# Where the transposes of a part stand in the first step of a graph attention layer

## The chip, the cores and the metric

The kernel runs on one core of a Trainium2 chip. A core has five engines that run beside each other and wait for each other through semaphores: TensorE (PE, matmuls and transposes), VectorE (DVE), ScalarE (ACT), GpSimd (POOL) and SyncE (SP, which issues most of the transfers). The metric is the time of the whole program on the device in microseconds, the median of several runs. Beside it there is one profiled execution, from which all rows of the trace come.

## The reference

The input is a table `x` of N = 3327 nodes with 256 features and a sparse weighted adjacency `adj`. A normalised and rectified copy h of x goes through two steps. In each, attention sums rows with the weights of a nucleus (top-p) softmax, and the adjacency diffuses a second copy:

```python
R = S + eye(N);  R = R / R.sum(-1)
Z = 0;  Xf = Xa = h
for n in range(2):
    q, k = Xa @ W1.T @ W2.T, Xa @ W3.T
    p = softmax(q @ k.T)                     # N x N
    mask = the largest p of a row, until their sum reaches 0.9
    A = p * mask / (p * mask).sum(-1)
    Xf = R @ Xf
    Xa = A @ Xa
    Z = Z + Xf @ U1[n].T + Xa @ U2[n].T
out = x + layernorm(h + Z)
```

Everything is float32.

## The kernel before

**Tiles.** The nodes are padded to 26 tiles of 128 rows (NT = 26). A tile of one step needs its row of weights, 128 x 3328 numbers in one of several buffers `e`. For tile t the work is, in order:

- `weights`: the queries (`project`, pq L526 and L528), the logits against all keys (pl L567) and their Exp on ACT (e L571 and L575).
- `measured`: on ACT, two long passes over e (ja L600) and small operations in columns of `g`, which guess a threshold.
- `settle`: on DVE, w (L700), the largest values of segments (L705), their merging, and at last the mask, which overwrites e with the kept weights (L734).
- `Sums`: the masked e is transposed in groups of four 128 x 128 blocks, and each group is multiplied with the rows of the table and added up in `pa`.
- in the first step `first_end`: the result times U2 (pz L889), its copies xw (L890) and sv (L892), and the next step's keys and queries (`prep`, pk L487).

Beside it the adjacency is read (`listed`: at L810, fm L811), the few neighbours of a row are found (`packed`, `gathered`: pb, po, lo, index), POOL gathers their rows (ac L859, xg L868), and `spread` multiplies them (pr L876).

**Sums.** A tile has PARTS = 7 groups, six of four blocks and one of two. `turn(g, made)` transposes groups until group g + ahead is done: PE writes a block of PSUM `pt` (L779), ACT copies it to SBUF as `eT` (L781). `sum(g)` multiplies group g (pa L793). After a tile's seventh group ACT takes pa out (xa L800). There are three buffers of eT. PSUM has two buffers of pt, and these serve pk, pq, pb, po, pg and the transposes of results as well; pa and pr have one buffer each.

**The order of the work.** The loop near the end of the kernel writes down one order for all engines. Its passes i go over the tiles, and each pass has seven parts k. In a part, the letters of `PLAN[step][k]` say which piece of which generator comes next:

```python
PLAN = (("mdsssa", "mdsssa", "edawwp", "sda", "mpdea", "mdgawwq", "emdgq"), ...)
LATE = (1, 4)
```

m is `measured` for tile i+1, d is `settle` for tile i, s is `spread` for tile i-2, e is `first_end` for tile i-2, w and q are `weights` of tiles ahead, a is `listed`, p is `packed`, g is `gathered`. With LATE = 1 in the first step, part k of pass i sums group 7(i-1) + k - 1. So parts 1 to 6 sum the first six groups of tile i-1, and part 0 sums the seventh of tile i-2. What is left of the generators is run at the end of a pass.

PE, ACT and DVE are tied to the order of this text: a dependency of each instruction on the one before it on its engine is added after the loop (IN_ORDER). SP and POOL are not in that list; their queues are ordered by the framework's planner.

Of the kernel before, what the change touches and what calls it, by code (L numbers as in the profile page):

```python
# [22 lines left out]
NT = (N + P - 1) // P  # L23
# [299 lines left out]
SQG, SQK = ((c[0], c[1] / (2 * c[0]), c[2] - c[1] ** 2 / (4 * c[0])) for c in (PG, PK))  # L323
HALF = NT // 2
PARTS = -(-NT // 4)
AHEAD = (1, 2)
COUNTED = [t for t in range(NT - 2) if t % 2 == 0]
EARLY = (11, 18, NT)
FIRST = 8 * P
# [14 lines left out]
def guess_graph_layer(ctx, tc, x, adj, w1t, w2t, w3t, u1t, u2t, ln_g, ln_b, out, flag):  # L344
# [207 lines left out]
    def weights(step, t, live, known=True):  # L552

        r = dict(Z=rec[:, step, 3, t : t + 1])
        qT, r["ms"] = yield from project(step, t, law=known)
        yield
        r["e"] = e = es[(2, 3, 0, 1, 4, 5)[t % 6] if step else t % 4]
        r["za"] = za = small.tile([P, CUT + 1], F32, tag="za", name="za")
        live[step, t] = r
        w = HALF * P  # L560
        wd = w // CUT
        for n in range(CUT):
            c = n * wd
            pl = ps_l.tile([P, 2, 512], F32, tag="pl", name="pl")
            for a in range(2):
                p = slice(a * DA, (a + 1) * DA)
                PE.matmul(pl[:, a, :wd], qT[p, :],  # L567
                          keys[step][p].rearrange("p a b -> p (a b)")[:, c : c + wd],
                          start=True, stop=True)
            if n < CUT - 1:  # L570
                S.activation(e.rearrange("p (a n) -> p a n", a=2)[:, :, c : c + wd], pl[:, :, :wd],  # L571
                             AF.Exp, accum_out=za[:, n : n + 1])
                yield
            else:
                S.activation(e.rearrange("p (a n) -> p a n", a=2)[:, :, c : w - 1], pl[:, :, : wd - 1],  # L575
                             AF.Exp, accum_out=za[:, n : n + 1])
                S.activation(e[:, w - 1 : w], pl[:, 0, wd - 1 : wd], AF.Exp, accum_out=za[:, n + 1 :])
# [110 lines left out]
    def measured(step, r):  # L688
        return measured_twice(r) if step else measured_once(r)
# [52 lines left out]
    def prove(step):  # L742
        v8, t, tn, Z = (rec[:, step, k, :] for k in range(4))
        ok = small.tile([P, NT], F32, tag="cum", name="ok", bufs=1)
        o2 = small.tile([P, NT], F32, tag="dr", name="o2", bufs=1)
        V.tensor_tensor(ok, v8, t, ALU.is_lt)
        V.tensor_tensor(o2, tn, t, ALU.is_lt)
        V.tensor_tensor(ok, ok, o2, ALU.mult)
        for a, c, op in ((tn, 0.0, ALU.is_gt), (t, 0.5 * BIG, ALU.is_lt),
                         (Z, 1.0e-30, ALU.is_gt), (Z, BIG, ALU.is_lt)):  # L750
            V.scalar_tensor_tensor(ok, a, c, ok, op, ALU.mult)
        V.tensor_scalar(ok, ok, 0.5, None, ALU.is_lt)
        n = N - (NT - 1) * P
        f = small.tile([P, 1], F32, tag="f", name="f")
        V.tensor_reduce(f, ok[:, : NT - 1], AX.X, ALU.add)
        V.tensor_tensor(fl, fl, f, ALU.add)
        V.tensor_tensor(fl[:n], fl[:n], ok[:n, NT - 1 :], ALU.add)
        if step == 0:
            V.tensor_scalar(ok, lists[:, :, LIST - 1], 0.0, None, ALU.is_gt)
            V.scalar_tensor_tensor(ok, ends, float(P), ok, ALU.is_gt, ALU.add)  # L760
            V.tensor_reduce(f, ok, AX.X, ALU.add)
            V.tensor_tensor(fl, fl, f, ALU.add)
# [121 lines left out]
    def first_end(t):  # L884
        aT = transposed(live.pop(("r", t)))
        yield
        pz = ps_r.tile([P, 2 * D], F32, tag="pr", name="pz")
        for c in range(ND):
            PE.matmul(pz, aT[:, c, :], u2[:, c].rearrange("p n d -> p (n d)"), start=c == 0, stop=c == ND - 1)  # L889
        S.copy(xw[:, t, :], pz[:, D:])  # L890
        sv = row.tile([P, D], F32, tag="sv", name="sv", bufs=2)
        V.tensor_tensor(sv, pz[:, :D], x0[:, t, :], ALU.add)  # L892
        nc.sync.dma_start(sx[t], sv)
        yield
        yield from prep(1, aT, t)
# [32 lines left out]
    def run(work, n=99):  # L928
        for _ in range(n):
            next(work, None)  # L930

    def returned(work):
        while True:
            try:
                next(work)
            except StopIteration as end:
                return end.value[1]
# [52 lines left out]
    def spread(step, t):  # L990
        rr = rrs[:, t : t + 1]
        own = row.tile([P, D + 1], F32, tag="own", name="own", bufs=2)
        nc.sync.dma_start(*((own[:, :D], vx[:, t, :]) if step else (own, bx[:, t, :])))
        s1 = row.tile([P, D], F32, tag="s1", name="s1", bufs=4)
        nc.sync.dma_start(s1, (sx if step else ax)[t])
        a, w = acs.pop(t), D + 1 - step
        pr = yield from diffuse(a, xgs.pop(t), own[:, :w], w)
        if step == 0:
            nc.sync.dma_start(cx[t], a.rearrange("p k r -> p (k r)"))
        yield  # L1000
        if step == 0:
            V.reciprocal(rr, pr[:, D : D + 1])
        V.scalar_tensor_tensor(s1, pr[:, :D], rr, s1, ALU.mult, ALU.add)  # L1003
        if step == 0:
            nc.sync.dma_start(vx[:, t, :], s1)
        else:
            live["f", t] = s1
# [20 lines left out]
    for step in range(2):  # L1028
        sums = Sums(step, live, xw if step else x0, AHEAD[step])

        for i in range(-1, NT + 2):
            if step == 0 and i == NT - 3:
                begun = [weights(1, t, live, False) for t in range(3)]
            if step == 1 and i == -1:
                run(begun[0])
                prove(0)
                for e in es[4:]:
                    G.memset(e[:, N:NP], 0.0)
            work.update(
                n=work["m"],  # L1040
                c=work["d"],
                d=settle(step, i, live[step, i]) if valid(i) else none,
                m=measured(step, live[step, i + 1]) if valid(i + 1) else none,
                s=spread(step, i - 2 + 2 * step) if valid(i - 2 + 2 * step) else none,
                w=later.pop((step, i + 2), none),
                e=first_end(i - 2) if step == 0 and valid(i - 2) else none,
                a=lister if step == 0 and i else none,
                p=packed(i + 1) if step == 0 and i >= 0 and valid(i + 1) else none,
                g=none if not valid(i + 2 * step) else refetch(i + 2) if step else gathered(i),
                b=none, q=none, v=proof() if step and i == NT else none,  # L1050
            )
            if i >= 0 and valid(i + 3):
                later[step, i + 3] = weights(step, i + 3, live)
                work["q"] = itertools.islice(later[step, i + 3], 2)
            if step == 0 and i >= NT - 2 and i < NT + 1:

                work["w"] = itertools.islice(begun[i - NT + 2], CUT - 1)
            if step == 0 and i >= NT - 3 and i < NT:
                work["q"] = itertools.islice(begun[i - NT + 3], 1)
            if i == -1:  # L1060
                work["w"] = itertools.chain(begun[1], begun[2])
            if step == 0 and i < 1:
                work["b"] = itertools.islice(product, EARLY[i + 2] - EARLY[i + 1])
            if step == 1 and i == -1:
                work["g"] = itertools.chain(refetch(0), refetch(1))
            for k in range(PARTS):
                g = PARTS * (i - 1) + k - LATE[step]
                summing = valid(g // PARTS)
                if summing:
                    sums.turn(g, min(i, NT - 1))  # L1070
                for c in "bb" + (LAST.get(i, PLAN[1]) if step else PLAN[0])[k]:
                    next(work[c], None)
                if summing:
                    ended = sums.sum(g)
                    if ended and step == 0:
                        live["r", ended[0]] = ended[1]
                    elif ended:
                        work["f"] = finish(ended[0], live.pop(("f", ended[0])), ended[1])
            for c in "cnwqsepgb" if step else "dmwqsepgb":
                run(work[c])  # L1080
            if step == 0 and i == NT:
                moments(1)
                for t in range(3):
                    live[1, t]["ms"] = returned(project(1, t, queries=False))
# [50 lines left out]
```

## Time and profile before

| what | value |
|---|---|
| median of 9 runs | 1559.59 us (1552.86 to 1566.1) |
| the profiled execution | 1566.31 us, its span 1564.5 us |
| PE busy over the span | 1332.0 us, 85% |
| DVE busy | 1230.9 us, 79% |
| ACT busy | 1104.6 us, 71% |
| POOL busy | 1003.7 us, 64% |
| mean granted clock of TensorE | 0.945 |

The first step's tiles run until about 900 us; then comes the second step. In a row of the trace the line names the source, `out<-in` the tiles it writes and reads, and x the number of instructions. A float32 matmul appears as two records, so a sum of four blocks is `x8`; a transpose is one record. The brackets at the end of a row give the idle time of the engine before it and what ended that. Ends of matmuls are modelled, so rows that follow each other on PE overlap by some tenths of a microsecond.

### The profile page before, as it was taken

To read this page: it belongs to the slowest core of one execution; us is meant where nothing else is said; L and a number is where in the kernel's file an instruction comes from. 1 tells how busy PE (TensorE), PEld (TensorE's weight loads), DVE (VectorE), ACT (ScalarE), POOL (GpSimd) and SP (SyncE) were. 2 spreads that over 40 slices of the span, in tenths; PEclk is the share of its full clock that TensorE was granted. 3 is DMA by queue.
4 is the path that set the end of the run, shared out by engine and by line. 5 is a ranking of instruction groups with operands and counts; after the bars stand their busy time and mean duration, and the time that the engine had idled before them with its cause. 6 is when DMAs were issued, how large, how long until landed. Compare 5 with 4: busy or idle time off the path is not lost.

```text
span 1564.5 us, 22648 instructions
## 1 busy us (share of the span) xinstructions
PE 1332.0 (85%) x6495; PEld 997.5 (64%) x6495; DVE 1230.9 (79%) x3837; ACT 1104.6 (71%) x2476; POOL 1003.7 (64%) x1489
## 2 busy tenths in 40 slices
PE   5857788988988988989999946989989998998886
PEld 3523666666766666767767724767767667676675
DVE  4457789779779778779787229989888899898894
ACT  5527566766766766766775368988988988988951
POOL 6312466555566555565575166888888888888851
PEclk9978899998999999998999978999999999999998
DMA  7554344343444444344332231221221221222200
GB/s 218 166 161 134 102 130 121 109 122 117 111 128 120 116 117 116 112 127 120 110 88 81 60 88 31 72 75 55 74 72 50 82 64 58 82 60 63 81 18 20
DMA packets 97687, 149.81 MB, mean 96 GB/s; under 512 B 15985, under 2 KB 60528, under 8 KB 97552
## 3 DMA queue, kind: packets, MB, share of 16 engines
q1 hardware_dynamic: 78400, 104.00, 21.7%
q0 software_dynamic: 16640, 42.69, 11.0%
q10 hardware_dynamic: 2512, 1.57, 0.4%
q8 instruction: 54, 0.88, 0.2%
q14 instruction: 81, 0.66, 0.2%
HBM read 120.93 MB, written 27.28 MB: 95 GB/s over the span
## 4 chain that ended last, share of the span: by engine, by line
PE 33%; POOL 23%; ACT 19%; DVE 11%; issue 8%; DMA 4%; another core or an unknown queue 1%; SPq 0%; ACTq 0%; POOLq 0%; DVEq 0%
PE pa L793 14%; ACT ja L600 8%; POOL xg L868 8%; POOL g L678 4%; PE pt L779 4%; PE pr L876 4%; PE pl L567 4%; DMA at<-in_adj 3%; ACT e L571 3%; ACT eT L781 2%; PE pz L889 2%; DVE e L734 2%; DVE fm L811 1%; PE pk L487 1%; POOL rstd L468 1%
## 5 line engine op out<-in xcount | busy, mean ns | idle before, releaser
L781 ACT COPY eT<-pt 128x512 f32<-128x512 f32 (+1 forms) x364 | 201.9, 556 | 225.2 <-PE pt L779 136.6
L793 PE MATMUL pa<-x,eT 128*128 128x256 f32 x1352 | 356.0, 408 | 5.3 <-ACT eT L781 3.1
L793 PE MATMUL pa<-xw,eT 128*128 128x256 f32 x1352 | 331.1, 387 | 30.5 <-ACT xa L800 30.0
L859 POOL DMA_INDIRECT ac<-in_adj,index x130 | 173.6, 1335 | 243.0 <-DVE mq L541 158.6
L600 ACT ACTIVATE ja<-e,g 128x3328 uint8<-128x3328 f32 x106 | 325.8, 3074 | 0.1
L793 PEld LDWEIGHTS pa<-xw,eT 128*128 128x128 f32 x1352 | 249.3, 191 | 92.9 <-ACT xa L800 35.0
L793 PEld LDWEIGHTS pa<-x,eT 128*128 128x128 f32 x1352 | 263.7, 203 | 61.2 <-issue 16.5
L705 DVE MAX8 cand<-w 128x8 f32<-128x168 f32 (+1 forms) x1040 | 251.3, 319 | 0.0
L779 PE MATMUL pt<-ident,e 128*128 128x128 f32 x1144 | 181.4, 279 | 39.7 <-DVE e L734 24.0
L868 POOL DMA_INDIRECT xg<-bx,index x130 | 178.8, 1375 | 47.5 <-issue 33.8
L779 PEld LDWEIGHTS pt<-ident,e 128*128 128x128 f32 x1144 | 144.9, 145 | 79.2 <-issue 32.1
L567 PE MATMUL pl<-k,qT 64*128 64x416 f32 x832 | 185.5, 550 | 4.4 <-ACT qT L531 3.9
L700 DVE SCALAR_TENSOR_TENSOR w<-e,g 128x3328 f32<-128x3328 f32 x44 | 164.0, 3727 | 0.7
L876 PE MATMUL pr<-xg,ac 128*128 128x257 f32 (+1 forms) x520 | 138.3, 389 | 23.4 <-DVE s L1003 20.1
L811 DVE TENSOR_REDUCE fm<-at 128x4 f32<-128x512 f32 (+1 forms) x182 | 115.9, 638 | 53.7 <-DMA at<-in_adj 50.8
L868 POOL DMA_INDIRECT xg<-vx,index x130 | 128.5, 989 | 43.8 <-issue 36.9
L734 DVE SCALAR_TENSOR_TENSOR e<-e,rec 128x3328 f32<-128x3328 f32 x40 | 147.1, 3678 | 0.0
L571 ACT ACTIVATE e<-pl 128x832 f32<-128x832 f32 x132 | 113.4, 867 | 8.1 <-PE pl L567 6.7
L876 PEld LDWEIGHTS pr<-xg,ac 128*128 128x128 f32 x520 | 91.0, 195 | 34.1 <-DVE s L1003 20.4
L567 PEld LDWEIGHTS pl<-k,qT 64*128 64x128 f32 x832 | 70.8, 188 | 50.7 <-issue 42.1
L712 DVE MAX8 bb<-cand 128x8 f32<-128x160 f32 x286 | 92.8, 324 | 6.4
L892 DVE TENSOR_TENSOR sv<-pz,x 128x256 f32<-128x256 f32 x26 | 11.0, 421 | 97.3 <-ACT xw L890 94.4
(226 smaller groups left out, 2226.4 us busy)
## 6 DMA issues: line engine op xcount, KB each, us to landing
at<-in_adj SPq DMA_DIRECT2D x156, 256.0 KB
cx<-ac SPq DMA_DIRECT2D x26, 384.0 KB
ac<-cx SPq DMA_DIRECT2D x26, 384.0 KB
bx<-e SPq DMA_DIRECT2D x26, 128.5 KB
own<-bx SPq DMA_DIRECT2D x26, 128.5 KB
x<-in_x SPq DMA_DIRECT2D x13, 256.0 KB
xr<-in_x SPq DMA_DIRECT2D x26, 128.0 KB
ax<-e SPq DMA_DIRECT2D x26, 128.0 KB
```

Source lines behind the costliest of these rows:

```text
L567: PE.matmul(pl[:, a, :wd], qT[p, :], keys[step][p].rearrange("p a b -> p (a b)")[:, c : c + wd], start=True, stop=True)
L571: S.activation(e.rearrange("p (a n) -> p a n", a=2)[:, :, c : c + wd], pl[:, :, :wd], AF.Exp, accum_out=za[:, n : n + 1])
L600: S.activation(ja, e, f, bias=guess, scale=sign, accum_out=total)
L700: V.scalar_tensor_tensor(w, e, col(16), e, ALU.is_lt, ALU.mult, accum_out=d2)
L705: V.max(cand[:, 8 * s : 8 * s + 8], w[:, s * SEG : min(NP, (s + 1) * SEG)])
L734: V.scalar_tensor_tensor(e, e, at(1), e, ALU.is_ge, ALU.mult, accum_out=ra)
L779: PE.transpose(pt[:, j, :], e[:, (j0 + j) * P : (j0 + j + 1) * P], ident)
L781: S.copy(eT[:, :w, :], pt[:, :w, :])
L793: PE.matmul(self.pa, eT[:, c - 4 * k, :], self.xa[:, j, :], start=c == 0, stop=c == NT - 1)
L859: G.indirect_dma_start(out=ac[:, k, :], out_offset=None, in_=rows, in_offset=bass.IndirectOffsetOnAxis(ap=index[:, t, k : k + 1], axis=0), ...
L868: G.indirect_dma_start(out=xg[:, k, :w], out_offset=None, in_=rows, in_offset=bass.IndirectOffsetOnAxis(ap=index[:, t, k : k + 1], axis=0))
L876: PE.matmul(pr[:, :w], ac[:, k, :], own if k == KT - 1 else xg[:, k, :w], start=k == 0, stop=k == KT - 1)
```

## The change

In the first step the call of `turn` moves from the beginning of a part to behind the letters of the part, directly in front of the part's sum, and the transposes run two groups ahead of the sum and no longer one. In the second step both stay as they are. At the end of a pass, what is left of the generators now comes after both the transposes of the next tile's first group and the sum.

```diff
-AHEAD = (1, 2)
+AHEAD = (2, 2)
...
             for k in range(PARTS):
                 g = PARTS * (i - 1) + k - LATE[step]
                 summing = valid(g // PARTS)
-                if summing:
+                if summing and step:
                     sums.turn(g, min(i, NT - 1))
                 for c in "bb" + (LAST.get(i, PLAN[1]) if step else PLAN[0])[k]:
                     next(work[c], None)
+                if summing and not step:
+                    sums.turn(g, min(i, NT - 1))
                 if summing:
                     ended = sums.sum(g)
```

## The prediction

> **What bounds the kernel now.** I read the page first, then sums over the steady part of the first step (200 to 900 us), then who waited for whom there, then the chain of waits through a tile, and last the rows of single engines.
>
> ```profile
> span 1564.5 us, 22648 instructions
> PE 1332.0 (85%) x6495; PEld 997.5 (64%) x6495; DVE 1230.9 (79%) x3837; ACT 1104.6 (71%) x2476; POOL 1003.7 (64%) x1489
> 200.00:900.00 700.00, 626.94 (x3075) 476.15 (x3073) 552.44 (x1762) 458.19 (x1115) 400.94 (x510) 0.95 0.39 111
> L487 PE MATMUL pk<-xT,wk x100: 275/275/582, 208.5 to 896.0; 128*128 128x128 f32 x100
> ...
> DVE sv L892 <- ACT xw L890: 94.4, 15, 9.9
> ACT eT L781 <- PE pt L779: 92.0, 57, 5.2
> ACT eT L781 <- remote: 27.8, 10, 5.2
> PE pq L526 <- ACT eT L781: 39.8, 20, 2.9
> ```
>
> The page's second line has the busy shares of the whole span. The third line, from the view by windows, gives busy time in a stretch of 700 us: PE 627, DVE 552, ACT 458, POOL 401, at a granted clock of 0.95. No engine fills the stretch; PE has 73 us left. The fourth line, from the view of one source line, gives the cadence: four key matmuls per tile, so 25 tiles and 24 intervals from 208.5 to 896.0 us, 28.6 us each. The waits go in a ring: ACT waits for PE's transposes, PE for ACT's copies, DVE for ACT. Such a ring is shortened only by what stands in it, and the chain of waits shows it (start, length, what):
>
> ```profile
> 459.96 1.73 PE pa L793 x8
> 461.69 0.44 PE pt L779 x4
> 462.13 3.22 PE pz L889 x4
> ...
> 466.06 2.75 issue
> ...
> 469.01 0.26 ACT xw L890
> ...
> 472.17 0.85 ACT e L571 x2
> ...
> 474.40 0.71 PE pk L487 x4
> ```
>
> PE's sums and transposes lead up to ACT's long pass over a tile (L600, most of the 2.75 us called issue), then come xw, the Exp copies, and through mq the next tile's keys (pk) on PE. Call the seven groups of transposes of a tile T0 to T6 and their sums S0 to S6. Today's PE order in a tile is pk, S5 of the tile before, T0, S6 of the tile before, T1, S0, T2, S1, T3, S2, T4, pz, S3, T5, po, pl, pq, S4, T6, with the small products between. In the single rows of PE (one sum of four f32 matmuls is eight records) and ACT it looks like this:
>
> ```profile
> 532.59 0.71 PE L487 MATMUL pk<-xT,wk 128*128 128x128 f32 x4 [1.73 <-ACT mq L535]
> 533.14 1.89 PE L793 MATMUL pa<-x,eT 128*128 128x256 f32 x8
> ...
> 545.80 1.89 PE L793 MATMUL pa<-x,eT 128*128 128x256 f32 x8
> 547.53 0.60 PE L779 MATMUL pt<-ident,e 128*128 128x128 f32 x4
> 547.97 1.88 PE L889 MATMUL pz<-u,xT 128*128 128x512 f32 x4
> ...
> 551.41 0.60 PE L779 MATMUL pt<-ident,e 128*128 128x128 f32 x4
> ...
> 548.22 0.59 ACT L781 COPY eT<-pt 128x512 f32<-128x512 f32 x1 [1.63 <-issue]
> 548.70 3.07 ACT L600 ACTIVATE ja<-e,g 128x3328 uint8<-128x3328 f32 x1
> 551.77 0.36 ACT L890 COPY xw<-pz 128x256 f32<-128x256 f32 x1
> 555.90 0.59 ACT L781 COPY eT<-pt 128x512 f32<-128x512 f32 x1 [3.77 <-remote]
> ```
>
> ACT stands idle for 1.63 us until T4 is through, and T4 had to let S2 (545.80) pass. The long pass L600 stands behind the copy of T4 in ACT's queue, though it doesn't need it. The last row is a second thing: T5 ended at 552.01 (551.41 and 0.60), and its copy began 3.9 us later, with ACT idle for 3.77. PE's word that T5 is done came late.
>
> **The change part by part.** *Nothing is added or taken away*: the same transposes, copies and sums, no DMA, no new tile. SP and POOL get no instruction, and DVE keeps its order. On PE each T moves in front of one S. The new order is pk, T0, S5 before, T1, S6 before, T2, S0, T3, S1, T4, S2, pz, T5, S3, po, pl, pq, T6, S4. On ACT the copies change places with two small things only: the eviction xa now follows T1's copy, and the moments' copy gt follows T0's.
>
> *What is gained.* Between pk and the long pass, PE now has to do everything it did before except S2. So T4 comes one sum earlier, 1.73 us by the chain (1.89 by the row, whose end overlaps the next group). The copy of T4, L600 and, through xw, sv and mq, the next pk follow. The 1.63 us of ACT's idle time before T4's copy is the same amount seen from the other side. Is the gain given back within the tile? S2 falls behind T4, and xw also needs pz: T4 to the end of pz is 1.73 + 1.88 = 3.6 us, while the copy and L600 take 0.59 + 3.07 = 3.7 us. They come out level, so pz just doesn't take over. After xw, the gap to pk is ACT's (Exp, Ln and copies); T6 and S4 lie under it.
>
> *24 intervals of 1.73 us are 41.5 us.* Both ends: 0, if the late word sets the pace, and 73 us, PE's idle time in the stretch.
>
> *T6 before S4* makes T6 wait for ACT's copy of po earlier than it did, with S4 behind it. pk needs ACT's mq, which comes after two Exp copies (from 472.17 to pk at 474.40 in the chain, 2.2 us), and S4 needs 1.73 us: hidden. Without that cover it would cost 1.73 us a tile.
>
> *T0 before S5* puts a wait for DVE's mask (L734) ahead of a sum; behind it queue S5, the pr products and T1. The mask's rows:
>
> ```profile
> 527.50 0.42 DVE L892 TENSOR_TENSOR sv<-pz,x 128x256 f32<-128x256 f32 x1 [6.80 <-ACT xw L890]
> 528.43 3.68 DVE L734 SCALAR_TENSOR_TENSOR e<-e,rec 128x3328 f32<-128x3328 f32 x1
> ...
> 172.32 1.89 PE L793 MATMUL pa<-x,eT 128*128 128x256 f32 x8
> 181.71 1.09 PE L779 MATMUL pt<-ident,e 128*128 128x128 f32 x4 [7.50 <-DVE e L734]
> ```
>
> The mask ended at 532.1 (528.43 and 3.68) and pk at about 533.3, so T0 in its new place would have waited for nothing, with 1.2 us to spare. The last two rows show the one tile where it costs: at 172 us S5 ran while the mask was out; now it follows the mask. One sum, 1.73 us, once.
>
> *POOL and SP* are not held to the text's order, so the planner may place their work differently. The nearest rows are one gather and its issue gap, below: 0.95 + 0.30 = 1.25 us, either way, times 24 is 30 us to either side. I take 0, since nothing of theirs is edited.
>
> *PE's slow clock.* 0.95 granted over 700 us is 35 us lost. Fewer idle stretches could give some back, more could take some; I take 0 of it, bounds plus and minus 10 us as an estimate of under a third of those 35. [...]
>
> **Sum.** The profiled execution took 1566.3 us, 1.8 us of it outside the span: 1566.3 - 41.5 + 1.7 = 1526.5. It lies 6.7 us above the median of 1559.6, so the forecast for the median is 1520 us, its own range 1502 to 1538.
>
> **The rivals.**
> *The late word sets the pace.* The rows of POOL:
>
> ```profile
> 549.60 0.95 POOL L859 DMA_INDIRECT ac<-in_adj,index  x1 [0.31 <-issue]
> 550.85 0.95 POOL L868 DMA_INDIRECT xg<-bx,index  x1 [0.30 <-issue]
> ```
>
> Releases are late while this train of gathers is under way. If T4 or T5, even one sum earlier, still falls into that stretch, its copy starts when it did before. For it: 27.8 us of ACT's waits have no named releaser. Against it: the 1.63 us wait above is an ordinary one. If it holds in every second tile, 12 x 1.73 = 20.8 us are left: about 1540 us.
> *The T's slip out in front of the train.* T5 at 550.1 instead of 551.85 would be ahead of most of it, and its 3.77 us of idle time shrink too. Taking 2.9 us more in every second tile: 41.5 + 12 x 2.9 = 76, capped by PE's 73: about 1487 us.
> *It changes nothing*: pz, level with L600 to 0.1 us, or DVE takes the place of the pass. [...] Against it: DVE has 148 of 700 us idle, 94.4 of them waiting for xw. About 1559 us.
> *Slower: T0 holds PE up.* If DVE's mask comes over 1.2 us later relative to pk than in the rows above, T0 blocks, and S5, which covered the wait, is pushed out behind it: up to 1.73 us in each of 24 tiles, 41.5 us, decided once the mask ends later than pk. For it: DVE inserts a tile's list work between sv and the mask in some tiles, and at 172 us the mask was 7.5 us late. Against it: where DVE waited 6.80 us for xw, xw starts both the mask and the way to pk. Without the gain this is 1601 us, with half of each 1580 us; I put it at 1580. [...]
>
> **How the numbers follow.** Forecast 0.42; late word 0.20; slipping out 0.15; nothing 0.09; slower 0.14. 0.3% of the time is 4.7 us, what a measurement of this kernel tells from no change, so "same" is 1554.9 to 1564.3. Faster: 0.42 + 0.20 + 0.15 = 0.77. The range goes down to 1480, a little below the case of slipping out with some clock regained, and up to 1564, the end of "same". Left out are the slower case and a remainder of 0.05 below.
>
> **What would show it.** Right: the cadence of pk near 26.9 us; ACT's 1.63 us before T4's copy gone; DVE's 94.4 us for xw clearly less; a second step as long as before. The late word: idle time of 3 us still before the copies of T4 or T5. Slipping out: these gone, the cadence near 25.5 us. Slower: PE's transposes waiting for L734 in many tiles. My step fails if xw comes no earlier after pk, or if the gain shows up again as PE's wait at pk.

## The result and the profile after

The changed kernel took 1515.15 us (median of 19 runs, 1494.44 to 1549.54), the kernel before, run beside it, 1559.87 us (62 runs, 1552.86 to 1568.89). By the two medians the ratio is 0.971; the ratio of fast runs, which leaves out the eight of the 19 that lie over 1.5% above the quickest, is 0.9669, its 95% interval 0.9651 to 0.9688. The forecast was 1520 us. The profiled execution took 1497.3 us, near the quickest of the 19; that of before took 1566.3.

The page of the kernel after, its span and the busy shares:

```profile
span 1495.6 us, 22653 instructions
...
PE 1298.1 (87%) x6495; PEld 983.3 (66%) x6495; DVE 1229.1 (82%) x3837; ACT 1105.8 (74%) x2476; POOL 1023.8 (68%) x1489
```

DVE and ACT did the same work as before (1230.9 and 1104.6 us), PE 34 us less of busy time for the same matmuls. The cadence of the keys, from the view of line L487, has the same 25 tiles as before:

```profile
L487 PE MATMUL pk<-xT,wk x100: 272/275/421, 209.0 to 828.7; 128*128 128x128 f32 x100
```

It is 619.7 / 24 = 25.8 us, where it was 28.6. From the last key to the end it is 1495.6 - 828.7 = 666.9 us, before 1564.5 - 896.0 = 668.5: the second step is 1.6 us shorter, and nearly the whole difference lies in the first. The view by windows, 200 to 800 us, first before and then after (length, busy time of PE, PE's weight loads, DVE, ACT and POOL, then the granted clock):

```profile
200.00:800.00 600.00, 533.82 (x2606) 404.94 (x2605) 496.22 (x1577) 404.58 (x992) 354.60 (x456) 0.94 0.41 117
```

```profile
200.00:800.00 600.00, 562.06 (x2916) 437.52 (x2915) 544.65 (x1739) 448.85 (x1085) 421.61 (x507) 0.99 0.45 126
```

Per tile, PE's busy time is 533.82 / 600 x 28.65 = 25.5 us before and 562.06 / 600 x 25.82 = 24.2 after; its idle time is 3.2 and 1.6 us. So of the 2.8 us that a tile got shorter in this pair, 1.5 are waiting and 1.3 are the same work at a granted clock of 0.99 instead of 0.94. The waits in the same stretch (total, times, longest), before and after:

```profile
DVE sv L892 <- ACT xw L890: 68.6, 11, 7.3
...
PE pq L526 <- ACT eT L781: 37.3, 19, 2.9
...
PE pk L487 <- ACT mq L535: 23.3, 16, 2.4
```

```profile
PE pt L779 <- ACT lo L846: 32.0, 22, 1.9
...
DVE sv L892 <- ACT xw L890: 19.7, 5, 4.9
...
ACT lo L846 <- PE pq L528: 17.0, 10, 2.3
...
PE pq L526 <- ACT eT L781: 5.8, 5, 1.6
```

PE's waits for mq are gone and those for eT nearly so; a new one has come, of the transposes for lo. One tile of after shows where. First ACT's rows, then PE's:

```profile
509.93 0.58 ACT L781 COPY eT<-pt 128x512 f32<-128x512 f32 x1 [1.38 <-PE pt L779]
510.41 3.07 ACT L600 ACTIVATE ja<-e,g 128x3328 uint8<-128x3328 f32 x1
...
513.48 0.36 ACT L890 COPY xw<-pz 128x256 f32<-128x256 f32 x1
513.81 0.58 ACT L781 COPY eT<-pt 128x512 f32<-128x512 f32 x1
...
518.94 0.17 ACT L846 COPY lo<-po 128x13 f32<-128x13 f32 x1 [2.19 <-PE pq L528]
```

```profile
513.12 0.60 PE L779 MATMUL pt<-ident,e 128*128 128x128 f32 x4
...
515.29 0.29 PE L844 MATMUL po<-lists,oh 128*128 128x13 f32 x2
...
519.17 0.44 PE L779 MATMUL pt<-ident,e 128*128 128x128 f32 x2 [1.55 <-ACT lo L846]
...
521.34 0.71 PE L487 MATMUL pk<-xT,wk 128*128 128x128 f32 x4
```

T5 (513.12) reaches ACT at once, and its copy at 513.81 follows xw without a wait; before, that copy stood 3.77 us. But po, done on PE at 515.58, is copied to lo only at 518.94. The late word is still there. In this tile it strikes lo instead of T5, and behind it T6, placed ahead of S4, waits 1.55 us. It is not so everywhere: by ACT's rows between 200 and 800 us, lo's copy waits 0.7 to 2.5 us in eleven of 23 tiles, T5's still 0.8 to 3.3 us in ten, T4's 2.8 to 5.2 us in three. ACT's ordinary wait before T4's copy, 1.63 us before, is still 1.38.

### The profile page after: what moved, and what is told of

Same layout as the page of the kernel before. It is cut to its first block, busy times and chain, and to the rows that moved or that the text cites. A ratio compares the mean times of both kernels' runs of the same rounds, so it can differ in the third digit from the quotient of the medians.

```text
span 1495.6 us, 22653 instructions
## 1 busy us (share of the span) xinstructions
PE 1298.1 (87%) x6495; PEld 983.3 (66%) x6495; DVE 1229.1 (82%) x3837; ACT 1105.8 (74%) x2476; POOL 1023.8 (68%) x1489
## 4 chain that ended last, share of the span: by engine, by line
PE 41%; POOL 24%; ACT 13%; DVE 10%; issue 6%; DMA 5%; another core or an unknown queue 0%; SPq 0%; POOLq 0%; ACTq 0%; DVEq 0%
PE pa L793 18%; POOL xg L868 8%; ACT ja L600 6%; PE pt L779 5%; PE pl L567 5%; POOL g L678 5%; PE pr L876 4%; DMA at<-in_adj 3%; PE pz L889 2%; ACT eT L781 2%; ACT e L571 2%; DVE e L734 1%; DVE cand L705 1%; PE pk L487 1%; POOL rstd L468 1%
## 5 line engine op out<-in xcount | busy, mean ns | idle before, releaser
L793 PE MATMUL pa<-xw,eT 128*128 128x256 f32 x1352 | 330.9, 386 | 29.2 <-ACT xa L800 28.6
L793 PE MATMUL pa<-x,eT 128*128 128x256 f32 x1352 | 332.2, 388 | 0.0
L600 ACT ACTIVATE ja<-e,g 128x3328 uint8<-128x3328 f32 x106 | 325.4, 3070 | 0.1
L859 POOL DMA_INDIRECT ac<-in_adj,index x130 | 197.0, 1516 | 153.7 <-DVE mq L541 105.6
L793 PEld LDWEIGHTS pa<-x,eT 128*128 128x128 f32 x1352 | 249.5, 195 | 27.9
L734 DVE SCALAR_TENSOR_TENSOR e<-e,rec 128x3328 f32<-128x3328 f32 x40 | 147.2, 3679 | 0.0
L600 ACT ACTIVATE ja<-x,g 128x3328 uint8<-128x3328 f32 x24 | 73.9, 3077 | 0.0
```

Source lines behind the costliest of these rows:

```text
L600: S.activation(ja, e, f, bias=guess, scale=sign, accum_out=total)
L734: V.scalar_tensor_tensor(e, e, at(1), e, ALU.is_ge, ALU.mult, accum_out=ra)
L793: PE.matmul(self.pa, eT[:, c - 4 * k, :], self.xa[:, j, :], start=c == 0, stop=c == NT - 1)
L859: G.indirect_dma_start(out=ac[:, k, :], out_offset=None, in_=rows, in_offset=bass.IndirectOffsetOnAxis(ap=index[:, t, k : k + 1], axis=0), ...
```

## The experiments

**One half of the change at a time.** The first two kernels undo one half each: transposes in front of the part but two groups ahead, and behind the letters but one ahead. The next two move one group, T4, behind the letters, or all but that one.

In e1, against before:

```diff
-AHEAD = (1, 2)
+AHEAD = (2, 2)
```

In e2, against after:

```diff
-AHEAD = (2, 2)
+AHEAD = (1, 2)
```

In e3, against before, with the edit of e1 and this one; e4 has `(0, 1, 2, 4, 5, 6)` in place of `(3,)`:

```diff
                 if summing:
+                    sums.ahead = AHEAD[step] if step else 1
                     sums.turn(g, min(i, NT - 1))
...
+                if summing and not step and k in (3,):
+                    sums.ahead = 2
+                    sums.turn(g, min(i, NT - 1))
```

> Two groups ahead, but the transposes stay at the head of the part. T4 then precedes S2 here too, and T0 stands in front of the keys pk, at the beginning of part 6. Theory of the ring (one sum less between pk and the long pass): the ring is as short as in the changed kernel, so 1505 to 1525 us, if T0 finds the mask ready. Rival that T0 holds PE up: the mask ended half a microsecond before pk in the trace of before, so T0 in front of pk would wait about as long as pk itself did and pk would be pushed out by T0's 0.44 us and S4's cover; 1530 to 1580 us. If place alone mattered (directly in front of the sum) and not the number of groups: 1560 us.

> The transposes directly in front of the sum, but only one group ahead. PE reaches the sums later relative to the copies, and ACT's copy of T4 now follows the long pass and xw. Theory of the ring: the pass waits for T3 instead of T4, the way from pk to it is no longer than in the changed kernel, 1505 to 1530 us. Theory of the late word (PE's signals come late while POOL's gathers are under way): the copy of T4 stands between xw and the Ln and Exp on the way to pk and falls into the late stretch, 2 to 4 us per tile are lost again, 1545 to 1600 us.

> Of all groups only T4 changes places with its sum (it goes in front of S2); the six others stand as in the kernel before. Theory of the ring: the whole gain of one sum per tile, 24 x 1.73 = 41 us, is here: 1515 to 1530 us. Theory that the gain comes from slipping out in front of the late stretch with T5: T5 stands where it stood, so at most half of the gain, 1535 to 1560 us.

> All groups but T4 change places with their sums; T4 stays behind S2. Theory of the ring: no gain, 1555 to 1565 us. Theory of slipping out: T5 still comes one sum earlier and leaves the late stretch in every second tile, 12 x 2.9 = 35 us, 1515 to 1540 us.

Measured: e1 1490.41 us (1.0044, 1.0029 to 1.0058), e2 1479.71 (0.9963, 0.9948 to 0.9977), e3 1483.74 (0.9994, 0.9979 to 1.001), e4 1486.36 (1.0014, 1.0004 to 1.0024). But the kernel *before*, unchanged, took 1484.07 us beside them (26 runs, 1480.62 to 1490.67) and not 1560. All four orders lie within half a per cent of it. What follows is that the theory of the ring can't be tried against 1560 us here, and that something other than the order makes 76 us of difference.

**Both kernels again, unchanged.** On another chip, to see what the pair is worth when before takes 1484 us.

> The kernel before, unchanged, for its trace on the chip where the comparison is made. In the four runs so far PE's signals were never late, the kernel before took 1484 us there, and no order of the transposes moved that by more than 0.5%. Theory that the late signal is what the edit repairs: where the signals are prompt this takes about 1484 us, key matmuls every 25.3 us, no idle time of 3 us before a copy; where they are late it takes about 1560 us again, with bunched signals once a tile. Theory of the ring (a late signal has no part in it): 1560 us in both cases.

> The changed kernel, unchanged, beside the one before on one chip. Theory of the late signal: where signals are prompt, within 0.5% of the kernel before (1477 to 1491 us); where they are late, 40 to 55 us faster. Theory of the ring: about 40 us faster in both cases.

Measured: before 1483.0 us (against further runs of itself 0.9987, 0.9973 to 1.0002), after 1481.4 (0.9975, 0.9962 to 0.9989). The change is worth about 3.5 us here and not 45. The windows of before in this run, and its cadence by the view of one line:

```profile
200.00:800.00 600.00, 573.22 (x3002) 446.41 (x3004) 552.35 (x1764) 453.73 (x1101) 427.34 (x510) 1.00 0.45 130
```

```profile
L487 PE MATMUL pk<-xT,wk x100: 274/275/378, 209.5 to 812.8; 128*128 128x128 f32 x100
```

PE is busy for 573 of 600 us and DVE for 552, at a clock of 1.00, and a tile takes 603.3 / 24 = 25.1 us. The rows of ACT show why the ring of the prediction is not what cost the time:

```profile
556.03 0.58 ACT L781 COPY eT<-pt 128x512 f32<-128x512 f32 x1 [1.64 <-PE pt L779]
556.51 3.07 ACT L600 ACTIVATE ja<-e,g 128x3328 uint8<-128x3328 f32 x1
...
561.14 0.58 ACT L781 COPY eT<-pt 128x512 f32<-128x512 f32 x1 [1.20 <-PE pt L779]
```

The wait of 1.64 us before T4's copy is there as in the trace of the slower before, although the kernel needs 76 us less. What is missing is the long wait before T5's copy.

e3 says it more directly. With T4 in front of S2, its copy waits in none of the 23 tiles, and xw comes sooner after the key, as the prediction had it: 18.2 us after pk, where it is 19.5 in e5 (means between 200 and 790 us). But from xw to the next pk it takes 7.2 us instead of 5.7, so that a tile stays at 25.4 us against 25.3. Behind xw ACT now waits for T5, and PE's wait at pk is still there:

```profile
506.83 0.36 ACT L890 COPY xw<-pz 128x256 f32<-128x256 f32 x1
508.90 0.59 ACT L781 COPY eT<-pt 128x512 f32<-128x512 f32 x1 [1.70 <-PE pt L779]
...
514.12 0.71 PE L487 MATMUL pk<-xT,wk 128*128 128x128 f32 x4 [1.01 <-ACT mq L535]
```

The record of semaphore events shows where the late word stands. For one tile, the end of each group on PE as modelled and the time at which PE's semaphore counted it:

```
before, 1566 us:   pz  549.85   T5  552.01   po  552.14   pl 553.04 553.74   counted: 555.82 555.86 555.92 555.98
e5, 1484 us:       T4  555.94   pz  558.89   T5  561.05   po  561.18   pl 562.08 562.77   counted: 555.96 558.90 561.06 561.19 562.10 562.80
```

In e5 each count follows its end by 0.01 to 0.03 us; signals are called prompt below where it is so, and late where it is not. In the first row four counts come within 0.16 us. There are five ends to them, and the count that is missing from the record is pz's: xw waits on PE's semaphore for pz, and it began at 551.77. So the four belong to T5, po and the two pl, and they come 3.8 to 2.2 us after the ends. As the ends are modelled, it stays open whether the work or its count was late. Between 200 and 800 us there are 21 such bunches of two or more counts, at most 0.07 us from one to the next, in before and 25 in after, in the pair of the result; in each of e1 to e6, whose profiled executions took 1480 to 1492 us, there are none.

In before they strike T5 in every second tile, whose copy then mostly waits 2.9 to 3.9 us, and T4 itself in most of the others, where its copy waits 2.4 to 5.2 us. The late word is PE's: in the same tile the counts of ACT and DVE that are on record follow their ends by 0.02 us or less. Others of theirs are missing (1561 of 1752 of ACT's and 1808 of 2218 of DVE's are on record in before, in e5 all of them), so the number of bunches is rough.

POOL's gathers run beside PE in both, in before and in e5. Beside the two rows of before that the prediction shows (549.60 and 550.85) these of e5 look alike:

```profile
559.59 0.94 POOL L859 DMA_INDIRECT ac<-in_adj,index  x1 [0.30 <-issue]
560.83 0.95 POOL L868 DMA_INDIRECT xg<-bx,index  x1 [0.30 <-issue]
```

So a train of gathers is where the bunches stand, but isn't enough to make them. In the six traces that have bunches, the pair of the result and e7 to e10, each of the 148 comes at one place of a train: 1.0 to 1.6 us after the end of its last gather, or within that gather where it takes 3.5 to 4.4 us instead of 0.95. There are two trains a tile and about one bunch.

In e6 the condition of the rival that ends slower is met. The waits and PE's row:

```profile
PE pt L779 <- DVE e L734: 27.4, 19, 2.3
```

```profile
493.01 0.63 PE L779 MATMUL pt<-ident,e 128*128 128x128 f32 x4 [1.87 <-DVE e L734]
```

T0 waits for the mask in 19 tiles, 27.4 us in all, and the kernel is 3.5 us faster and not 41 slower. The way from pk to xw is 19.3 us, as long as in e5 (19.5), though one sum left it: the wait for the mask takes most of its place. PE is busy for 570 us of 600 in e6 and DVE for 553, which leaves an order little to win; that this is why the wait costs so little was not tried.

**DVE made lighter.** With prompt signals DVE seemed to hide the ring. The two kernels take work off DVE: of each load of the adjacency only one block of 128 columns is searched for neighbours, instead of up to four, and the others count as empty, so most neighbours are left out of the diffusion. The same edit is made to before (e7) and after (e8).

```diff
-                V.tensor_reduce(fm[:, j0 : j0 + n], at[:, :n], AX.X, ALU.max, apply_absolute_value=True)
+                if j0 == 0:
+                    V.memset(fm, 0.0)
+                V.tensor_reduce(fm[:, j0 : j0 + 1], at[:, :1], AX.X, ALU.max, apply_absolute_value=True)
```

> The kernel before with less work on DVE: the search for neighbours (fm) reduces one block of 128 columns per load instead of four, some 0.45 us less in six of seven reductions, about 2.8 us of DVE time per tile. The other blocks count as empty, so most neighbours are left out of the diffusion. On the chips with prompt signals DVE is busy 552 of 600 us in the first step (PE 573). Theory that DVE sets the pace there: 20 to 60 us less than the kernel before, until PE takes over, about 1430 to 1465 us. Theory that PE or ACT sets it: within 1% of the kernel before.

> The same with the changed order (the same part of the computation is left out). Theory of the ring, its gain being hidden by DVE so far: now 15 to 25 us faster than the light kernel with the order before, which keeps 1.0 us of PE's waiting for mq per tile, 24 x 1.0 = 24 us. Theory that the order only repairs late signals: within 0.5% of it.

Here the signals were late again: the kernel before took 1567.39 us (12 runs, 1557.54 to 1579.18), on the chip on which e1 to e4 had run beside 1484.07. So the lateness doesn't belong to a chip. Measured: e7 1557.84 us (0.993, 0.9894 to 0.9967), e8 1551.91 (0.9869, 0.9791 to 0.9947). The windows of e7, and the windows and waits of e8:

```profile
200.00:800.00 600.00, 532.96 (x2599) 403.91 (x2600) 456.05 (x1603) 405.40 (x987) 354.50 (x466) 0.94 0.49 117
```

```profile
200.00:800.00 600.00, 543.90 (x2651) 423.24 (x2651) 460.75 (x1622) 413.90 (x1000) 354.36 (x473) 0.92 0.50 119
```

```profile
DVE sv L894 <- ACT xw L892: 68.9, 15, 7.6
ACT eT L781 <- PE pt L779: 46.8, 26, 6.7
...
PE pt L779 <- ACT lo L848: 35.5, 21, 2.0
```

Two things follow. Where signals are late DVE doesn't set the pace: 40 us less of its work in 600 bring 10 us. And the order of the change brings 5.9 us between e7 and e8, no more than the noise of these runs (e8 is four runs, 1533.97 to 1554.06 us) and far from 45, although T4 has its new place: DVE waits 68.9 us for xw again, there are 32 bunches, and T4's copy itself waits 2.6 to 6.7 us in twelve of 20 tiles. By the ring a lighter DVE could only have helped; by the late word the gathers, which DVE's lists start, now come at another time relative to T4, T5 and lo, and strike them. The traces show the shift: the last gather of the train behind pz starts 5.3 us after pz in the middle tile of after, and 3.2 us after it in e8. That the gain hangs on this phase is argued from the shift and the waits, and not separately tried.

**Waits put in by hand.** Idle passes on ACT stand in for the late word: in e9, against before, in front of T5's copy in odd tiles and of T4's in even ones (3.1 and 4.6 us); in e10, against after, half a pass of about 1.5 us in front of lo.

In e9, ahead of the copy to eT:

```diff
+                if self.step == 0 and 1 < t < NT - 1 and k == 4 + t % 2:
+                    ja = scan.tile([P, NP], U8, tag="ja", name="ja")
+                    S.activation(ja, e, AF.Copy)
+                    if k == 4:
+                        S.activation(ja[:, : NP // 2], keys[0].rearrange("p a b -> p (a b)"), AF.Copy)
```

In e10, ahead of the copy to lo:

```diff
+        if 1 < t < NT - 1:
+            ja = scan.tile([P, NP], U8, tag="ja", name="ja")
+            S.activation(ja[:, : NP // 2], keys[0].rearrange("p a b -> p (a b)"), AF.Copy)
```

> The kernel before with ACT held up by idle passes where the first trace shows it waiting for PE's late signals: in front of the copy of T5 in odd tiles (one pass over e, 3.1 us) and of T4 in even ones (one and a half, 4.6 us, of which 1.6 are an ordinary wait). If such stretches alone make the difference between 1484 and 1560 us: 1540 to 1580 us on a chip with prompt signals. If ACT has slack there, because DVE sets the pace: less than 30 us more, below 1515 us.

> The changed kernel with ACT held up where its trace shows late signals: in front of the copy lo, half a pass, about 1.5 us in each tile but four. If the late signals cost the changed kernel what its trace suggests, 1495 to 1515 us; PE then waits at T6 for lo, with S4 and pk behind it. If there is slack: within 0.5% of the changed kernel's 1481 us.

Measured beside the same 1567.39 us: e9 1592.59 (1.0194, 1.0127 to 1.026), e10 1599.9 (1.0228, 1.0168 to 1.0287). The signals were late by themselves, so the passes came on top of what they were to stand in for, and e9 says only that most of the added time fell into waits that were there anyway: 11 x 3.1 + 12 x 4.6 = 89 us put in over 23 tiles (83 by ACT's busy time, 1187.7 against 1104.6), 25 us paid (1592.59 - 1567.39). e10 says more. In its waits:

```profile
DVE sv L895 <- ACT xw L893: 92.1, 18, 7.1
...
PE pt L779 <- ACT lo L849: 62.1, 20, 3.5
```

Some 1.5 us in front of lo in each of 23 tiles, 32 us by ACT's busy time (1137.9 against 1105.8), and the time is 1600 us, where after took 1515 in the result. T6's wait for lo doubles, DVE's wait for xw is longer than it was before the change (92.1 against 68.6 us), and the gain is lost altogether. The 1515 us are from another session, so the size of the loss is rough. Against the slowest run of after, 1549.54 us, it is still 50 us, more than was put in; no run of after stood beside e10.

**T4 left behind once more, and a version without the two new waits.** e11 is e4 again, to tell T4 from T5 and lo where signals are late. e12 puts only T1 to T5 in front of the sum, leaves T6 behind S4 and T0 behind S5, and runs the queries' pieces of the sixth part before the logits'.

```diff
-AHEAD = (1, 2)
+AHEAD = (2, 2)
-    PLAN = (("mdsssa", "mdsssa", "edawwp", "sda", "mpdea", "mdgawwq", "emdgq"),
+    PLAN = (("mdsssa", "mdsssa", "edawwp", "sda", "mpdea", "mdgaqww", "emdgq"),
...
+                    sums.ahead = AHEAD[step] if step else 1
                     sums.turn(g, min(i, NT - 1))
...
+                if summing and not step and k in (0, 1, 2, 3, 4):
+                    sums.ahead = 2
+                    sums.turn(g, min(i, NT - 1))
```

> Every group of transposes but T4 goes in front of the sum, as in the change; T4 alone stays behind S2, in front of the long pass L600. The run of the kernel before beside it tells which of two cases this is. If that one takes about 1560 us (PE's signals come late): by the ring of waits the whole gain of 41 us hangs on T4, so nothing is gained here, 1550 to 1570 us; by the other theory, T5 and lo being ahead of the stretch in which signals come late, most of the 45 us is kept, 1510 to 1530 us. If the one before takes about 1484 us, both theories give 1481 to 1488 us, and the run tells nothing new.

> T1 to T5 go in front of the sum as in the change, T6 and T0 stay as before, so that neither S4 waits behind T6 for lo nor S5 behind T0 for the mask; and in the sixth part the next tile's queries come before its logits. If PE's signals are late (the one before at about 1560 us): PE's 32 us of waits at T6 for lo and 17 us of ACT's for pq go in part, some 20 us under the change's 1515 us, 1485 to 1505 us; if the phase between POOL's gathers and PE decides instead, the queries' earlier place can lose the gain again, 1530 to 1560 us. If signals are prompt (about 1484 us): by DVE's 92% of busy time in the first step not more than 10 us, 1474 to 1484 us; if PE's waits for mq and the mask set the pace there, 24 tiles of 1.0 us at pk, about 1460 us.

The kernel before took 1485.09 us beside them: prompt. Measured: e11 1487.14 us (1.0006, 0.9989 to 1.0022), e12 1480.78 (0.9973, 0.9959 to 0.9987). e11 tells nothing new, as its expectation says for this case. e12 takes PE's waits at pk and T6 away and gains 4 us, like after in e6; its waits show what is late next:

```profile
PE pz L889 <- DVE s L1003: 19.2, 17, 2.1
```

PE, freed from waiting for ACT, waits for DVE. With prompt signals none of the orders tried took less than about 1480 us (e2, e6 and e12). Whether e12 beats after where signals are late was not seen.

## Why the prediction was right in size and wrong in cause

**The sum.** 41.5 us were to come from T4 reaching ACT one sum earlier. With prompt signals the same edit gives 3.5 us (e6), T4 alone 0.3 and within the interval of nothing (e3); with late ones and another phase 5.9, within the noise (e7 to e8). So the step that failed is the last link of "the copy of T4, L600 and, through xw, sv and mq, the next pk follow". In e3 xw comes 1.4 us earlier after pk, and the next pk doesn't follow: the way from xw to it is 1.5 us longer, with 1.70 us of waiting for T5. The prediction counted that way as ACT's own work and put no wait in it. In the pair of the result xw comes earlier too: from pk to xw it is 22.1 us before and 18.6 after on average. Some 1.8 us of that are the sum that left (19.2 and 17.4 in the shortest tiles, which no late word struck ahead of xw); the rest are late words. From xw to the next pk it is 7.1 and 7.4, where before's tiles without a late word behind xw have 5.5.

That "the 1.63 us of ACT's idle time before T4's copy is the same amount seen from the other side" was a misreading too. T3 moves up together with T4, and a sum (S1 instead of S2) still stands between them, so the wait is 1.38 us in after, 1.64 in the prompt before. Where it does go, in e3, nothing is gained. What held the tiles of before up were the late words: the 3.77 us before T5's copy, which the prediction called "a second thing" and left to a rival, and 2.4 to 5.2 us before T4's copy in most of the tiles between. Most of the 45 us are time won back from them: the kernel takes 1484 us without late signals, loses 76 to them, and after the change loses 1515 - 1481 = 34. That the forecast came within 5 us of the result was luck.

**The clock** was taken as 0, at most 10 us. It gave 1.3 us a tile, 24 x 1.3 = 31 us of the 69 between the two profiled executions. The granted clock is 0.94 with the waits of before, 0.99 with those of after and 1.00 in e5, where PE is idle for 66, 38 and 27 of the 600 us. No wait of PE between 200 and 800 us is longer than 2.9 us in before and 1.9 us in after; what brought the clock down is not shown. The term left at 0 was the second largest.

**pz level with L600** was right: in the tile shown pz ended at 513.28 (511.40 and 1.88, by its row), the pass made way for xw at 513.48, and xw waited for neither. In five of the 23 tiles xw did wait, 7.8 us in all.

**T6 before S4, "hidden"** by the Exp copies, was wrong where signals are late: the copies themselves stand behind lo in ACT's queue, and lo was late. PE's waits came to 32.0 us in 22 tiles. With prompt signals e6 shows no more than 0.2 us of them. This is a cover that goes away together with the condition it was read under.

**T0 before S5** was right for the result: no wait for L734 in the stretch. With prompt signals the wait came (27.4 us in e6), as the rival said, but without its price.

**POOL and SP, nothing; the second step as long as before:** right, by the totals (668.5 and 666.9 us). POOL's order differs in small places through the first step (gsum, and the addition to ac at L856, change places with a neighbour); no run tried it by itself.

**The rivals.** "The T's slip out in front of the train" is what the rows show in part: T5's wait gone in the tile shown, the cadence of 25.8 us near this rival's 25.5 and not at the forecast's 26.9, ten of the 24 intervals between 24.9 and 25.6 us. (Its working takes 551.85 for T5, which is po's start; T5 started at 551.41.) It was given 0.15 and 1487 us, and the quickest runs of after come near that. "The late word sets the pace" is the other half: it went on to strike lo and T6. Between the two, 1540 and 1487, lies 1515. After spreads over 55 us where before spread over 16; that what is struck changes from run to run would explain it, but only one of these executions of after has a trace.

**What stays open.** Why PE's counts come late in some sessions and not in others. It isn't the chip's number (one chip had both), nor the kernel (before had both), nor the gathers alone (they run in both). Whether taking the gathers away removes the bunches was not tried in a session that had them. And the direct test of T4 against T5 and lo with late signals was not had, so how much of the 45 us each of them brought is not known.

## What to carry to other kernels

When a row says that an engine sat idle though its releaser had long ended, price that wait first and run the kernel before once more before reasoning on it: a large gain may only be the repair of a disturbance that other sessions don't have. A wait that stands in the chain is not yet what holds the tile up; ask whether the same wait is there when the kernel runs faster. An order that wins by phase against another engine's transfers is worth what the phase is worth: in e10 about 1.5 us more in front of lo went with the loss of the whole gain (1599.9 us, where after took 1515.15 in another session).

## What the runs showed of the hardware

PE's completions, as counted by its semaphore, came 0.01 to 0.03 us after the modelled end in the tile of e5 shown above, and 3.8 us after it for T5 in the tile of before. In the middle one of before's 21 bunches the first count came after 3.2 us, if a bunch holds the last ends ahead of it. In the tile of before that is shown four counts came within 0.16 us of each other; 21 bunches in 600 us are about one per tile of 28.65 us, and they come 1.0 to 1.6 us after the end of a train of indirect gathers, or within its last gather where that takes 3.5 to 4.4 us. Of the profiled executions, the six of 1497 us and more (the pair of the result, e7 to e10) have 20 to 32 such bunches between 200 and 800 us, the eight of 1480 to 1492 (e1 to e6, e11, e12) have none. The same unchanged kernel took 1484 us in some sessions and 1560 to 1567 in others, on one chip in both ways.

PE's granted clock was 0.94 between 200 and 800 us of before, where no wait of PE is longer than 2.9 us, and 0.89 in e10, where waits of up to 3.5 us come once a tile. In e5, where none is longer than 1.2 us, it is 1.00. The longest wait doesn't settle it: e6 has one of 2.3 us and 1.00, e8 none over 2.0 us and 0.92.
